# A two-layer recurrence on one core: all gates by ScalarE from PSUM, state copies and one forget product on VectorE, own places for the variances, another order

## The chip, the cores and the metric

The kernel runs on one core of one Trainium2 chip. The metric is the device time of one execution in microseconds (us); less is better.

## What is computed

The input is an image of 256 x 256 positions with 32 channels. Four layers follow each other, each adding to the image: an attention block (here only its value and gate paths matter, since the softmax runs over an axis of length 1), two Sobel layers, and a recurrent network. Each layer first normalizes the image by groups of channels. The change concerns the fourth layer alone. It reads the image as 256 sequences (rows) of 256 steps (columns), with a hidden size of 128 and two layers:

```
def step(carry, x_t):
    h_all, c_all = carry
    z = x_t @ W_lat + b_lat
    for j in range(L):
        zz = jnp.concatenate([z, h_all[j]], axis=1) @ W_cell[j] + b_cell[j]
        zz = _group_norm(zz, gn_gamma[j], gn_beta[j])
        i, f, o, g = jnp.split(zz, 4, axis=1)
        c = jax.nn.sigmoid(f) * c_all[j] + jax.nn.sigmoid(i) * jnp.tanh(g)
        h = jax.nn.sigmoid(o) * jnp.tanh(c)
        z = z + h
        ...
    x_hat = x_t + z @ W_out + b_out
```

The group norm has four groups of 128, which are the four gates, so each gate has its own mean and standard deviation per sequence. All data are float32.

## The kernel before

The first 640 us or so hold the input, the attention layer and the two Sobel layers. The change doesn't touch them.

The recurrence takes the rest. The 256 sequences are two halves of 128, one sequence per partition. So each time step has four units of work: layer `l` (0 or 1) and half `h` (0 or 1), written (0, 0), (0, 1), (1, 0) and (1, 1). The weights are centred beforehand, so the four gates' means are zero and only a variance is left to compute. Each unit consists of these parts, by the names of the program:

- `x` (line 763): the input's share of `zz`, a PSUM tile of 128 x 512 with all four gates, from `fx`. The function `project` issues it; two of them, for a unit of layer 0 and one of layer 1, are issued as a pair. Every unit has one PSUM buffer, so the next `x` of a unit has to wait until the last reader of its `zz` is done.
- `i` (line 788), for layer 1: adds layer 0's new state. `m` (line 793): adds the unit's own state of the step before.
- `sq` (line 801): ScalarE squares `zz` from PSUM. `rd` (line 806): VectorE sums the squares of each gate into `ve`. `pw` (line 809): GpSimd raises `ve` to the power -0.5; the result is `rs`, 1/std of four gates per sequence.
- `nz`, `n2` (line 773), for layer 0: VectorE multiplies `zz` by `rs`, in two halves of 256 columns, into `zn` in SBUF.
- The gates `ga`. In layer 0 ScalarE reads `zn`: `sg` (line 837) does two sigmoids at once, `so` (line 839) the third, `tg` (line 841) the tanh. In layer 1 ScalarE reads `zz` from PSUM with `rs` as the scale, one instruction for each gate (line 782).
- `ig` (line 844): VectorE multiplies input gate and tanh. `fc` (line 848): GpSimd multiplies forget gate and old `c`. `c` (line 852): VectorE adds the two. `th` (line 856): ScalarE takes tanh. `h` (line 859): VectorE multiplies by the output gate.
- `T` (line 864): TensorE transposes `h` into PSUM. `e` (line 869): the copy into `hT`, by VectorE in layer 0 and by ScalarE in layer 1. `hs` (line 874): GpSimd adds both layers' `hT` for the output.

After every block of four steps the output follows (`emit`): `px` from `xa` (line 880) and from `hs` (line 883) on TensorE, `fin` on ScalarE (line 891), a transpose `st` on VectorE (line 894), and four DMAs on SP's queue. SP also loads the next inputs, `xt`, well ahead.

The order of the instructions is written out by hand. `PLAN` gives each part of a unit a due time, and `PERIOD` is added for each step; `EMIT` does the same for the output. All parts of all steps are sorted by due time and issued in that order. The times serve for sorting only: each engine takes its own instructions in that order, and each waits for what it needs. An engine never overtakes.

There is a second arm of the program for general gamma and beta of the group norm, chosen at run time. With these inputs it isn't taken.

Of the kernel before, what the change touches and what calls it, by code (L numbers as in the profile page):

```python
# [10 lines left out]
F32 = mybir.dt.float32  # L11
AF = mybir.ActivationFunctionType
# [5 lines left out]
T = 256  # L18
C = 32
J = 4  # L20
NB = T // J
P = 128
H = 128
L = 2
# [633 lines left out]
class RecurrentInputs:  # L658
# [40 lines left out]

PERIOD = 8.665
PLAN = {
    (0, 0): dict(m=0.0, sq=1.54, rd=2.25, pw=3.0, nz=4.22, n2=4.58, sg=5.22, tg=5.54, fc=5.7),
    (0, 1): dict(m=4.42, sq=5.96, rd=6.66, pw=7.42, nz=8.53, n2=8.88, sg=9.47, tg=9.79, fc=9.95),
    (1, 0): dict(x=9.85, i=11.2, m=12.21, sq=13.35, rd=13.99, pw=14.81, nz=15.89, tg=15.9, so=16.2),
    (1, 1): dict(x=13.95, i=15.37, m=16.46, sq=17.59, rd=18.25, pw=19.07, nz=20.29, tg=20.3),
}
PLAN[0, 0].update(ig=5.95, c=6.4, so=6.5, th=6.75, h=7.28, T=7.65, e=8.01)
PLAN[0, 1].update(ig=10.2, c=10.65, so=10.75, th=11.0, h=11.53, T=12.06, e=12.62)  # L710
PLAN[1, 0].update(si=16.5, sg=16.8, ig=16.96, fc=17.27, c=17.89, th=18.66, h=19.09, T=19.71, e=20.07)
PLAN[1, 1].update(si=20.59, so=20.89, ig=21.05, sg=21.2, fc=21.66, c=22.25, th=23.08, h=23.51)
PLAN[1, 1].update(T=23.88, e=24.29, hs=30.77)
EMIT = 35.52


def recurrence(tc, out, ident, weights, inputs, general):

    nc = tc.nc
    wc, fx, e4, cst4, wout = weights  # L720
    sqs = inputs.sqs
    ctx = ExitStack()
# [15 lines left out]
                    nc.scalar.copy(dst[:, l, :], pb)  # L738

    up = ctx.enter_context(tc.tile_pool(name="unit", bufs=5))  # L740
    sp = ctx.enter_context(tc.tile_pool(name="state", bufs=2))
    hp = ctx.enter_context(tc.tile_pool(name="hid", bufs=6))
    op = ctx.enter_context(tc.tile_pool(name="outp", bufs=2))
# [6 lines left out]
    v = {}  # L750
    todo = []

    def at(when, what, *args):
        todo.append((when, len(todo), what, args))
# [10 lines left out]
    def one(name, l, h, t):  # L765
        seqs = slice(h * P, (h + 1) * P)
        get = lambda k: v[k, l, h]
        gates = lambda x, g: x[:, g * H : (g + 1) * H]
        four = lambda x: x.rearrange("p (g m) -> p g m", g=4)

        def half(i):
            g = slice(2 * i, 2 * i + 2)
            nc.vector.tensor_mul(  # L773
                four(get("zn"))[:, g, :],
                four(get("zz"))[:, g, :],
                get("rs")[:, g].unsqueeze(2).to_broadcast([P, 2, H]),
            )

        def gate(g, func):

            x, scale = (get("zn"), 1.0) if general else (get("zz"), get("rs")[:, g : g + 1])
            nc.scalar.activation(gates(get("ga"), g), gates(x, g), func, scale=scale)  # L782

        if name == "x":
            project(0, 1 - h, t + 1 + h)
            project(1, h, t)
        elif name == "i":
            nc.tensor.matmul(  # L788
                get("zz"), lhsT=v["hT", 0, t][:, seqs], rhs=wc[:, l, 0, :], start=False, stop=t == 0
            )  # L790
        elif name == "m":
            if t:
                nc.tensor.matmul(  # L793
                    get("zz"),
                    lhsT=v["hT", l, t - 1][:, seqs],
                    rhs=wc[:, l, 1, :],
                    start=False,
                    stop=True,
                )
        elif name == "sq":  # L800
            nc.scalar.activation(  # L801
                sqs[l, h][:, :, 0:H], four(get("zz")), AF.Square, scale=float(H**-0.5)
            )
        elif name == "rd":
            ve = v["ve", l, h] = up.tile([P, 4], F32, name="ve")
            nc.vector.tensor_reduce(ve, sqs[l, h], AX.X, ALU.add)  # L806
        elif name == "pw":
            rs = v["rs", l, h] = up.tile([P, 4], F32, name="rs")
            nc.gpsimd.tensor_tensor(rs, get("ve"), inputs.mhalf, ALU.pow)  # L809
        elif name == "n2":  # L810
            if not general:
                half(1)
        elif name == "nz":
            if l == 0 or general:
                zn = v["zn", l, h] = up.tile([P, 4 * H], F32, name="zn")
            if l:
                v["ga", l, h] = up.tile([P, 4 * H], F32, name="ga")
            if not general:
                if l == 0:
                    half(0)  # L820
                return
            for g in range(4):
                nc.vector.scalar_tensor_tensor(
                    gates(zn, g),
                    gates(get("zz"), g),
                    get("rs")[:, g : g + 1],
                    gates(gam[:, l, :], g),
                    ALU.mult,
                    ALU.mult,
                )  # L830
            nc.vector.tensor_add(zn, zn, bet[:, l, :])
        elif l and name in ("si", "sg", "so", "tg"):
            g = ("si", "sg", "so", "tg").index(name)
            gate(g, AF.Tanh if name == "tg" else AF.Sigmoid)
        elif name == "sg":
            ga = v["ga", l, h] = up.tile([P, 4 * H], F32, name="ga")
            nc.scalar.activation(ga[:, 0 : 2 * H], get("zn")[:, 0 : 2 * H], AF.Sigmoid)  # L837
        elif name == "so":
            nc.scalar.activation(gates(get("ga"), 2), gates(get("zn"), 2), AF.Sigmoid)
        elif name == "tg":  # L840
            nc.scalar.activation(gates(get("ga"), 3), gates(get("zn"), 3), AF.Tanh)
        elif name == "ig":
            c = v["cn", l, h] = sp.tile([P, H], F32, name=f"c{l}{h}")
            nc.vector.tensor_mul(c, gates(get("ga"), 0), gates(get("ga"), 3))  # L844
        elif name == "fc":
            if t:
                fc = v["fc", l, h] = up.tile([P, H], F32, name="fc")
                nc.gpsimd.tensor_mul(fc, gates(get("ga"), 1), get("c"))  # L848
        elif name == "c":
            c = get("cn")  # L850
            if t:
                nc.vector.tensor_add(c, c, get("fc"))  # L852
            v["c", l, h] = c
        elif name == "th":
            th = v["th", l, h] = up.tile([P, H], F32, name="th")
            nc.scalar.activation(th, get("c"), AF.Tanh)  # L856
        elif name == "h":
            hh = v["h", l, h] = up.tile([P, H], F32, name="h")
            nc.vector.tensor_mul(hh, gates(get("ga"), 2), get("th"))  # L859
        elif name == "hs":  # L860
            both(t)
        elif name == "T":
            pt = v["pt", l, h] = ps_h.tile([P, 4 * H], F32, name="pt")
            nc.tensor.transpose(pt[:, 0:P], get("h"), ident)  # L864
        elif name == "e":
            if h == 0:
                v["hT", l, t] = hp.tile([P, S], F32, name=f"hT{l}")
            copy = nc.scalar.copy if l else nc.vector.tensor_copy
            copy(v["hT", l, t][:, seqs], get("pt")[:, 0:P])  # L869

    def both(t):

# [2 lines left out]

    def emit(blk, part):

        if part == 0:
            px = v["px"] = ps_x.tile([P, S], F32, name="px")
            nc.tensor.matmul(px, lhsT=e4, rhs=inputs.xa[:, blk, :], start=True, stop=False)  # L880
        elif part == 1:
            for j in range(J):
                nc.tensor.matmul(  # L883
                    v["px"][j * C : (j + 1) * C, :],
                    lhsT=wout,
                    rhs=v.pop(("hs", blk * J + j)),
                    start=False,
                    stop=True,
                )
            fin = v["fin"] = op.tile([P, S], F32, name="fin")  # L890
            nc.scalar.activation(fin, v["px"], AF.Identity, bias=cst4)
        else:
            st = op.tile([P, S], F32, name="st")
            nc.vector.transpose(st, v["fin"])
            for j in range(J):
                nc.sync.dma_start(
                    out=out_q[j, :, blk],
                    in_=st[j * C : (j + 1) * C].rearrange("p (q c) -> p q c", c=C),
                )

    for k in range(inputs.NX, NB // inputs.XT):
        at(((k - inputs.NX + 1) * inputs.XT * J + 2.0) * PERIOD, inputs.load, k)
    for h in range(2):
        at(-1e5, project, 0, h, 0)
    at(PLAN[1, 1]["x"] - PERIOD, project, 0, 0, 1)
    for t in range(T):
# [1 line left out]
            for name, when in ops.items():  # L908
                at(t * PERIOD + when, one, name, l, h, t)
    for blk in range(NB):  # L910
        for part in range(3):
            at((blk * J + J - 1 + part) * PERIOD + EMIT, emit, blk, part)
    todo.sort(key=lambda e: e[:2])
    with tc.manual_schedule():
        for _, _, what, args in todo:
# [43 lines left out]
```

## Time and profile before

| What | Value |
|---|---|
| Three runs | 2893.24, 2894.18, 2903.16 us; median 2894.18 |
| The profiled execution | 2892.63 us |
| Its span, from first to last instruction | 2890.8 us |
| Mean granted TensorE clock | 0.983 |
| Busy, 1500 to 2000 us: PE, VectorE, ScalarE, GpSimd | 486.1, 427.9, 414.7, 372.1 us |
| One matmul pass, `L793` (two passes are one float32 matmul) | 594 ns |
| `rs` on GpSimd, `L809` | 1016 ns |
| `ve` on VectorE, `L806` | 678 ns |
| `sq` on ScalarE, `L801` | 591 ns |
| A gate from PSUM with `rs` as scale, `L782` | 371 ns |

The profile names an engine PE (TensorE matmuls), PEld (TensorE weight loads), DVE (VectorE), ACT (ScalarE), POOL (GpSimd) or SP. A row of the groups gives the line, engine and operation, what it writes and reads with shapes, how often, the busy time in us and the mean in ns of one, and then the idle time of the engine just before it with what ended most of that. A line of the timeline gives start, time taken, engine, line and operation; equal neighbours are merged ("x4"), and then the time taken runs from the first start to the last end. Neighbours on an engine can overlap, so a row's mean can be longer than the distance to the next start. The chain of work that ended last is followed back from the last instruction; in its answer in order of time each piece has its start, its length and the name of who held it. "issue" there is time in which nothing shown was waited for.

### The profile page before, as it was taken

To read this page: it belongs to the slowest core of one execution; us is meant where nothing else is said; L and a number is where in the kernel's file an instruction comes from. 1 tells how busy PE (TensorE), PEld (TensorE's weight loads), DVE (VectorE), ACT (ScalarE), POOL (GpSimd) and SP (SyncE) were. 2 spreads that over 40 slices of the span, in tenths; PEclk is the share of its full clock that TensorE was granted. 3 is DMA by queue.
4 is the path that set the end of the run, shared out by engine and by line. 5 is a ranking of instruction groups with operands and counts; after the bars stand their busy time and mean duration, and the time that the engine had idled before them with its cause. 6 is when DMAs were issued, how large, how long until landed. Compare 5 with 4: busy or idle time off the path is not lost.

```text
span 2890.8 us, 40872 instructions
## 1 busy us (share of the span) xinstructions
PE 2754.4 (95%) x9561; PEld 993.9 (34%) x9561; DVE 2422.5 (84%) x6507; ACT 2274.8 (79%) x6961; POOL 1934.2 (67%) x2586
## 2 busy tenths in 40 slices
PE   7899898989999999999999999999999999999997
PEld 4433333333333333333333333333333333333332
DVE  6788798978888888888888888888888888888886
ACT  5477676758888888888888888888888888888886
POOL 2311375657777777777777777777777777777775
PEclk9899999989999999999999999999999999999999
DMA  3000000000000000000000000000000000000000
GB/s 133 1 1 1 16 1 1 1 22 6 16 13 12 12 12 12 12 12 12 12 12 14 12 12 12 12 12 12 12 12 12 12 12 12 13 13 16 7 5 7
DMA packets 94354, 38.53 MB, mean 13 GB/s; under 512 B 74852, under 2 KB 91269, under 8 KB 94104
## 3 DMA queue, kind: packets, MB, share of 16 engines
q1 hardware_dynamic: 93156, 34.67, 5.3%
q8 instruction: 79, 1.29, 0.2%
q14 instruction: 171, 1.40, 0.2%
q10 hardware_dynamic: 148, 0.86, 0.1%
q0 software_dynamic: 800, 0.30, 0.0%
HBM read 10.63 MB, written 8.39 MB: 7 GB/s over the span
## 4 chain that ended last, share of the span: by engine, by line
PE 44%; DVE 32%; POOL 12%; issue 7%; ACT 2%; POOLq 0%; DVEq 0%; ACTq 0%
DVE ve L806 14%; POOL rs L809 11%; PE zz L793 11%; DVE c L852 7%; PE zz L788 6%; PE zz L763 5%; DVE zn L773 4%; PE pv L279 4%; PE pg L452 4%; PE pg L412 3%; DVE c L844 3%; PE pt L864 3%; PE pg L303 2%; PE px L883 2%; PE pg L279 1%
## 5 line engine op out<-in xcount | busy, mean ns | idle before, releaser
L809 POOL TENSOR_TENSOR rs<-ve,mhalf 128x4 f32<-128x4 f32 x1024 | 1040.3, 1016 | 252.0 <-DVE ve L806 225.5
L793 PE MATMUL zz<-wc,hT 128*128 128x512 f32 x2040 | 962.2, 594 | 1.2 <-DVE hT L869 1.2
L801 ACT ACTIVATE sq<-zz 128x512 f32<-128x512 f32 x1024 | 605.4, 591 | 245.7 <-PE zz L793 240.3
L806 DVE TENSOR_REDUCE ve<-sq 128x4 f32<-128x516 f32 x1024 | 694.4, 678 | 9.9 <-ACT sq L801 9.5
L848 POOL TENSOR_TENSOR fc<-ga,c 128x128 f32<-128x128 f32 x1020 | 464.8, 456 | 333.4 <-ACT ga L837 313.3
L782 ACT ACTIVATE ga<-zz,rs 128x128 f32<-128x128 f32 x2048 | 585.0, 371 | 4.6 <-POOL rs L809 1.1
L763 PE MATMUL zz<-fx,xt 33*128 33x512 f32 x2048 | 585.2, 643 | 3.3 <-issue 1.9
L788 PE MATMUL zz<-wc,hT 128*128 128x512 f32 x1024 | 525.3, 595 | 0.0
L793 PEld LDWEIGHTS zz<-wc,hT 128*128 128x128 f32 x2040 | 361.0, 197 | 262.6 <-DVE hT L869 201.6
L844 DVE TENSOR_TENSOR c<-ga 128x128 f32<-128x128 f32 x1024 | 307.5, 300 | 156.3 <-ACT ga L782 98.3
L773 DVE TENSOR_TENSOR zn<-zz,rs 128x256 f32<-128x256 f32 x1024 | 386.2, 419 | 54.8 <-POOL rs L809 20.4
L864 PEld LDWEIGHTS pt<-ident,h 128*128 128x128 f32 x1024 | 142.3, 139 | 797.9 <-DVE h L859 748.9
L864 PE MATMUL pt<-ident,h 128*128 128x128 f32 x1024 | 323.7, 316 | 67.4 <-DVE h L859 40.8
L856 ACT ACTIVATE th<-c 128x128 f32<-128x128 f32 x1024 | 310.4, 303 | 79.6 <-DVE c L852 59.8
L852 DVE TENSOR_TENSOR c<-c,fc 128x128 f32<-128x128 f32 x1020 | 368.8, 362 | 3.1 <-POOL fc L848 2.0
L859 DVE TENSOR_TENSOR h<-ga,th 128x128 f32<-128x128 f32 x1024 | 290.2, 283 | 0.8 <-ACT th L856 0.8
L763 PEld LDWEIGHTS zz<-fx,xt 33*128 33x128 f32 x2048 | 156.6, 185 | 348.2 <-PE zz L793 309.0
L869 DVE COPY hT<-pt 128x128 f32<-128x128 f32 x512 | 147.5, 288 | 111.5 <-PE pt L864 111.5
L837 ACT ACTIVATE ga<-zn 128x256 f32<-128x256 f32 x512 | 208.7, 408 | 3.9 <-DVE zn L773 3.9
L297 DVE TENSOR_TENSOR o<-pv,sg 128x512 f32<-128x512 f32 x256 | 158.0, 679 | 46.5 <-PE pg L279 37.7
L874 POOL TENSOR_TENSOR hs<-hT,hT 128x256 f32<-128x256 f32 x256 | 186.0, 726 | 1.7 <-ACT hT L869 1.7
L788 PEld LDWEIGHTS zz<-wc,hT 128*128 128x128 f32 x1024 | 183.3, 219 | 2.3 <-issue 2.3
(143 smaller groups left out, 2745.6 us busy)
## 6 DMA issues: line engine op xcount, KB each, us to landing
xt<-xa SPq DMA_DIRECT2D x256, 64.0 KB, 2.0
nat<-in_x_dram SPq DMA_DIRECT2D x16, 512.0 KB, 7.1
out_dram<-st SPq DMA_DIRECT2D x256, 32.0 KB, 1.7
wc<-in_L_conv_W_cell_dram SPq DMA_DIRECT2D x2, 512.0 KB, 4.5
kt<-in_consts_dram ACTq DMA_DIRECT2D x1, 832.0 KB, 5.9
wv<-in_L_conv_Wv_dram POOLq DMA_DIRECT2D x4, 32.0 KB, 5.0
wg<-in_L_conv_Wg_dram POOLq DMA_DIRECT2D x4, 32.0 KB, 6.0
gamma<-in_L_conv_ln_gamma_dram POOLq DMA_DIRECT2D x4, 0.1 KB, 6.3
```

Of the source, the lines that this page charges most:

```text
L763: nc.tensor.matmul(zz, lhsT=x, rhs=fx[rows, l, :], start=True, stop=l == 0 and t == 0)
L773: nc.vector.tensor_mul(four(get("zn"))[:, g, :], four(get("zz"))[:, g, :], get("rs")[:, g].unsqueeze(2).to_broadcast([P, 2, H]),)
L782: nc.scalar.activation(gates(get("ga"), g), gates(x, g), func, scale=scale)
L788: nc.tensor.matmul(get("zz"), lhsT=v["hT", 0, t][:, seqs], rhs=wc[:, l, 0, :], start=False, stop=t == 0)
L793: nc.tensor.matmul(get("zz"), lhsT=v["hT", l, t - 1][:, seqs], rhs=wc[:, l, 1, :], start=False, stop=True,)
L801: nc.scalar.activation(sqs[l, h][:, :, 0:H], four(get("zz")), AF.Square, scale=float(H**-0.5))
L806: nc.vector.tensor_reduce(ve, sqs[l, h], AX.X, ALU.add)
L809: nc.gpsimd.tensor_tensor(rs, get("ve"), inputs.mhalf, ALU.pow)
L844: nc.vector.tensor_mul(c, gates(get("ga"), 0), gates(get("ga"), 3))
L848: nc.gpsimd.tensor_mul(fc, gates(get("ga"), 1), get("c"))
L852: nc.vector.tensor_add(c, c, get("fc"))
L864: nc.tensor.transpose(pt[:, 0:P], get("h"), ident)
```

## The change

- Layer 0 takes its gates as layer 1 did: four activations from `zz` in PSUM with `rs` as scale. `zn` with its two VectorE products falls away (in the arm that is taken), and so does the double sigmoid. The parts are now called `sf`, `si`, `so`, `tg` in all units, and their order differs from unit to unit.
- The output gate gets a tile of its own, `go`, with three buffers.
- `e` is done by VectorE in both layers. `fc` is done by VectorE in layer 1 and stays on GpSimd in layer 0.
- `ve` and `rs` get places of their own for 64 steps, in two tiles that are never given back, in place of five rotating buffers.
- The plan has new due times for everything, and the output's four parts have due times of their own (`OUT`), with `fin` split from the matmuls ahead of it.

```diff
-PERIOD = 8.665
+SLOTS = 64
+PERIOD = 8.700
 PLAN = {
-    (0, 0): dict(m=0.0, sq=1.54, rd=2.25, pw=3.0, nz=4.22, n2=4.58, sg=5.22, tg=5.54, fc=5.7),
-    (0, 1): dict(m=4.42, sq=5.96, rd=6.66, pw=7.42, nz=8.53, n2=8.88, sg=9.47, tg=9.79, fc=9.95),
-    (1, 0): dict(x=9.85, i=11.2, m=12.21, sq=13.35, rd=13.99, pw=14.81, nz=15.89, tg=15.9, so=16.2),
-    (1, 1): dict(x=13.95, i=15.37, m=16.46, sq=17.59, rd=18.25, pw=19.07, nz=20.29, tg=20.3),
+    (0, 0): dict(m=3.34, sq=3.72, rd=4.73, pw=5.61, ga=5.84, sf=5.86, so=6.12, fc=6.24),
+    (0, 1): dict(m=7.00, sq=7.12, rd=8.38, pw=8.64, ga=9.88, sf=9.90, si=10.02, tg=10.28),
+    (1, 0): dict(x=13.81, i=17.21, m=17.59, sq=18.47, rd=19.23, pw=19.73, ga=21.35, sf=21.37),
+    (1, 1): dict(x=20.62, i=21.50, m=22.38, sq=23.14, rd=24.02, pw=25.15, ga=25.26, sf=25.28),
 }
-PLAN[0, 0].update(ig=5.95, c=6.4, so=6.5, th=6.75, h=7.28, T=7.65, e=8.01)
-PLAN[0, 1].update(ig=10.2, c=10.65, so=10.75, th=11.0, h=11.53, T=12.06, e=12.62)
-PLAN[1, 0].update(si=16.5, sg=16.8, ig=16.96, fc=17.27, c=17.89, th=18.66, h=19.09, T=19.71, e=20.07)
-PLAN[1, 1].update(si=20.59, so=20.89, ig=21.05, sg=21.2, fc=21.66, c=22.25, th=23.08, h=23.51)
-PLAN[1, 1].update(T=23.88, e=24.29, hs=30.77)
-EMIT = 35.52
+PLAN[0, 0].update(tg=6.37, si=6.75, ig=7.38, c=8.01, th=8.26, h=8.76, T=9.02, e=10.40)
+PLAN[0, 1].update(fc=10.65, so=11.16, ig=11.28, c=11.54, th=12.17, h=12.55, T=12.92, e=15.19)
+PLAN[1, 0].update(so=21.75, si=22.00, tg=22.25, fc=22.63, ig=22.76, c=22.88, th=23.39, h=24.27)
+PLAN[1, 0].update(T=24.90, e=25.03)
+PLAN[1, 1].update(tg=26.54, si=26.67, so=26.79, ig=26.92, fc=27.05, c=27.55, th=28.31, h=28.81)
+PLAN[1, 1].update(T=29.69, e=30.58, hs=34.23)
+
+OUT = dict(o0=29.06, o1=54.28, of=55.29, ot=68.15)
...
+    kp = ctx.enter_context(tc.tile_pool(name="norm", bufs=1))
+    sums = kp.tile([P, 2 * L, SLOTS, 4], F32, name="ve")
+    roots = kp.tile([P, 2 * L, SLOTS, 4], F32, name="rs")
...
             x, scale = (get("zn"), 1.0) if general else (get("zz"), get("rs")[:, g : g + 1])
-            nc.scalar.activation(gates(get("ga"), g), gates(x, g), func, scale=scale)
+            if g == 2:
+                v["go", l, h] = up.tile([P, H], F32, name="go", bufs=3)
+            dst = get("go") if g == 2 else gates(get("ga"), g)
+            nc.scalar.activation(dst, gates(x, g), func, scale=scale)
...
         elif name == "rd":
-            ve = v["ve", l, h] = up.tile([P, 4], F32, name="ve")
+            ve = v["ve", l, h] = sums[:, 2 * l + h, t % SLOTS, :]
             nc.vector.tensor_reduce(ve, sqs[l, h], AX.X, ALU.add)
         elif name == "pw":
-            rs = v["rs", l, h] = up.tile([P, 4], F32, name="rs")
+            rs = v["rs", l, h] = roots[:, 2 * l + h, t % SLOTS, :]
             nc.gpsimd.tensor_tensor(rs, get("ve"), inputs.mhalf, ALU.pow)
...
-        elif l and name in ("si", "sg", "so", "tg"):
-            g = ("si", "sg", "so", "tg").index(name)
+        elif name in ("si", "sf", "so", "tg"):
+            g = ("si", "sf", "so", "tg").index(name)
             gate(g, AF.Tanh if name == "tg" else AF.Sigmoid)
-        elif name == "sg":
-            ga = v["ga", l, h] = up.tile([P, 4 * H], F32, name="ga")
-            nc.scalar.activation(ga[:, 0 : 2 * H], get("zn")[:, 0 : 2 * H], AF.Sigmoid)
-        elif name == "so":
-            nc.scalar.activation(gates(get("ga"), 2), gates(get("zn"), 2), AF.Sigmoid)
-        elif name == "tg":
-            nc.scalar.activation(gates(get("ga"), 3), gates(get("zn"), 3), AF.Tanh)
...
-                nc.gpsimd.tensor_mul(fc, gates(get("ga"), 1), get("c"))
+                eng = nc.vector if l else nc.gpsimd
+                eng.tensor_mul(fc, gates(get("ga"), 1), get("c"))
...
-            nc.vector.tensor_mul(hh, gates(get("ga"), 2), get("th"))
+            nc.vector.tensor_mul(hh, get("go"), get("th"))
...
-            copy = nc.scalar.copy if l else nc.vector.tensor_copy
-            copy(v["hT", l, t][:, seqs], get("pt")[:, 0:P])
+            nc.vector.tensor_copy(v["hT", l, t][:, seqs], get("pt")[:, 0:P])
...
     for blk in range(NB):
-        for part in range(3):
-            at((blk * J + J - 1 + part) * PERIOD + EMIT, emit, blk, part)
+        for part, when in OUT.items():
+            at((blk * J + J - 1) * PERIOD + when, emit, blk, part)
```

More of the change, by code (lines that the diff above doesn't have):

```diff
@@ L769, in one @@
         four = lambda x: x.rearrange("p (g m) -> p g m", g=4)
[L771 to L777, printed above, removed]
         def gate(g, func):
             x, scale = (get("zn"), 1.0) if general else (get("zz"), get("rs")[:, g : g + 1])
-            nc.scalar.activation(gates(get("ga"), g), gates(x, g), func, scale=scale)
+            if g == 2:
+                v["go", l, h] = up.tile([P, H], F32, name="go", bufs=3)
+            dst = get("go") if g == 2 else gates(get("ga"), g)
+            nc.scalar.activation(dst, gates(x, g), func, scale=scale)
         if name == "x":
@@ L804, in one @@
         elif name == "rd":
-            ve = v["ve", l, h] = up.tile([P, 4], F32, name="ve")
+            ve = v["ve", l, h] = sums[:, 2 * l + h, t % SLOTS, :]
             nc.vector.tensor_reduce(ve, sqs[l, h], AX.X, ALU.add)
         elif name == "pw":
-            rs = v["rs", l, h] = up.tile([P, 4], F32, name="rs")
+            rs = v["rs", l, h] = roots[:, 2 * l + h, t % SLOTS, :]
             nc.gpsimd.tensor_tensor(rs, get("ve"), inputs.mhalf, ALU.pow)
-        elif name == "n2":
+        elif name == "ga":
+            v["ga", l, h] = up.tile([P, 4 * H], F32, name="ga")
             if not general:
[L812 to L820, printed above, removed]
                 return
+            zn = v["zn", l, h] = up.tile([P, 4 * H], F32, name="zn")
             for g in range(4):
@@ L876, in emit @@
     def emit(blk, part):
-        if part == 0:
+        if part == "o0":
             px = v["px"] = ps_x.tile([P, S], F32, name="px")
             nc.tensor.matmul(px, lhsT=e4, rhs=inputs.xa[:, blk, :], start=True, stop=False)
-        elif part == 1:
+        elif part == "o1":
             for j in range(J):
@@ L889, in emit @@
                 )
+        elif part == "of":
             fin = v["fin"] = op.tile([P, S], F32, name="fin")
```

## The prediction, made before the result was known

> I call the four units of a time step A (layer 0, first half of the sequences), B (layer 0, second half), C and D (layer 1, first and second half).
>
> **What bounds the kernel now.** I read the page first: busy shares and the chain of work that ended last.
>
> ```profile
> PE 2754.4 (95%) x9561; PEld 993.9 (34%) x9561; DVE 2422.5 (84%) x6507; ACT 2274.8 (79%) x6961; POOL 1934.2 (67%) x2586
> ...
> PE 44%; DVE 32%; POOL 12%; issue 7%; ACT 2%; POOLq 0%; DVEq 0%; ACTq 0%
> DVE ve L806 14%; POOL rs L809 11%; PE zz L793 11%; DVE c L852 7%; PE zz L788 6%; PE zz L763 5%; DVE zn L773 4%; PE pv L279 4%; PE pg L452 4%; PE pg L412 3%; DVE c L844 3%; PE pt L864 3%; PE pg L303 2%; PE px L883 2%; PE pg L279 1%
> ```
>
> PE looks full, yet the chain goes as much through VectorE and GpSimd (ve, rs, c, zn) as through the recurrence's matmuls. The shares mix stages, so next the stretches: the recurrence runs from about 640 to 2866 us, evenly.
>
> ```profile
> 1500.00:2000.00 500.00, 486.11 (x1527) 169.71 (x1526) 427.86 (x1276) 414.74 (x1391) 372.13 (x517) 1.00 0.06 12
> ```
>
> The columns are PE, PEld, DVE, ACT, POOL, then the granted clock (1.00). In the groups of 1500 to 2366 us, ve stands 398 times in 866 us; at four a step that is 8.70 us per step, 34.8 per block of four steps. In the timeline a step without output takes 2000.13 to 2008.65 = 8.52. Then the chain in order of time, over half a step:
>
> ```profile
> 2008.69 0.41 DVE zn L773
> 2009.10 0.47 DVE c L852
> 2009.58 0.60 DVE ve L806
> ...
> 2010.52 0.28 DVE c L852
> 2010.80 0.61 DVE ve L806
> ...
> 2011.54 1.02 POOL rs L809
> 2012.56 0.02 issue
> ```
>
> It begins with zn at 2008.35 and ends with the other half's zn at 2012.58: 4.23 us, twice 8.46 a step. This loop is the bound: VectorE without a break from zn to ve (3.06), the hand-over (0.13), rs on GpSimd (1.02). PE isn't in it. How much PE has left is seen in its timeline, where the starts count and the modelled ends don't:
>
> ```profile
> 2000.88 1.13 PE L763 MATMUL zz<-fx,xt 33*128 33x512 f32 x4
> 2002.13 0.33 PE L864 MATMUL pt<-ident,h 128*128 128x128 f32 x1
> 2002.29 1.02 PE L788 MATMUL zz<-wc,hT 128*128 128x512 f32 x2
> 2003.15 0.30 PE L864 MATMUL pt<-ident,h 128*128 128x128 f32 x1
> 2003.29 1.88 PE L793 MATMUL zz<-wc,hT 128*128 128x512 f32 x4
> 2005.11 1.13 PE L763 MATMUL zz<-fx,xt 33*128 33x512 f32 x4
> ```
>
> A matmul of 512 columns is two passes; four passes in 1.88 with 0.59 for the last gives (1.88-0.59)/3 = 0.43 a pass, 0.86 a matmul. A transpose costs 0.16 (2002.13 to 2002.29). A pair of x matmuls takes 1.06 (656.41 to the transpose at 657.47, where it didn't wait) plus 0.09 ahead of it (2003.29 + 4 x 0.43 = 5.01 against 5.11). Per step: six matmuls 5.16, four transposes 0.64, two pairs 2.30: 8.10. A block adds px from xa, 0.43 (2858.11 to 2858.64 without the 0.09), and px from hs, 0.56 (2865.93 to 2866.49): 0.25 a step. So **PE needs 8.35 of 8.70 us**, and 0.35 x 256 = 90 us is all that any change off PE can win: about 2806.
>
> **What the Trainium skill says.** "SBUF — State Buffer", section "Who interferes with whom": a VectorE instruction with two SBUF inputs contends with a GpSimd instruction that reads SBUF, and the first to issue blocks the other for its whole length. The trace agrees: c at 2000.50 takes 0.55 beside hs (2000.18 to 2000.91) and ends 0.147 after it, against 0.28 alone; ve isn't affected (0.68). "ScalarE: Activation LUTs", section "What ACT_TABLE_LOAD costs": a [128,1] pointer operand adds about 93 ns, and back-to-back activations overlap by about as much. Here a gate with rs as scale takes 0.371 against 0.30 without, and four take 1.14, so (1.14-0.37)/3 = 0.26 apart (0.25 by their starts). "TensorE: Matmul & The Clock Gate", section "Architectural detail": TensorE pulls weight loads ahead of running matmuls. The trace agrees: a load for L793 at 2003.84 stands beside matmuls that run until 2004.15. So a wait that ends somewhat early costs PE nothing.
>
> **The change part by part.** Rows:
>
> ```profile
> L809 POOL TENSOR_TENSOR rs<-ve,mhalf 128x4 f32<-128x4 f32 x1024 | 1040.3, 1016 | 252.0 <-DVE ve L806 225.5
> L806 DVE TENSOR_REDUCE ve<-sq 128x4 f32<-128x516 f32 x1024 | 694.4, 678 | 9.9 <-ACT sq L801 9.5
> L848 POOL TENSOR_TENSOR fc<-ga,c 128x128 f32<-128x128 f32 x1020 | 464.8, 456 | 333.4 <-ACT ga L837 313.3
> L782 ACT ACTIVATE ga<-zz,rs 128x128 f32<-128x128 f32 x2048 | 585.0, 371 | 4.6 <-POOL rs L809 1.1
> L773 DVE TENSOR_TENSOR zn<-zz,rs 128x256 f32<-128x256 f32 x1024 | 386.2, 419 | 54.8 <-POOL rs L809 20.4
> L837 ACT ACTIVATE ga<-zn 128x256 f32<-128x256 f32 x512 | 208.7, 408 | 3.9 <-DVE zn L773 3.9
> ```
>
> Layer 0's gates from PSUM: VectorE loses 4 zn a step at 0.34 apart, 1.36. It gains two state copies (0.21 apart; row of L869, 288 ns) and two fc (as h, 283 ns, 0.20 apart): 0.82. Most of what leaves stood in the loop, and rs then releases ScalarE directly. The loop is gone.
>
> ScalarE: sixteen gates at 0.25, four sq at 0.49 (2000.13 to 2000.62), four tanh at 0.20 (2001.13 to 2001.33), fin 0.37/4: 6.9 a step, of 8.35. Lone gates between other activations aren't shown; bounds are 0.25 (as in a run) and 0.371 (no overlap). I take 0.25, since mixed neighbours overlap too (sq of 0.597 is followed after 0.49).
>
> GpSimd loses two fc (0.91): 5.7 left. VectorE's new fc costs 0.20 free, up to 0.55 if it meets hs; it saves layer 1 a hand-over. I take 0.20, on neither critical chain.
>
> Own places for ve and rs: one wait per rs where there were two in every second; ve's start to rs is 0.76 with one (2000.98 to 2001.73), 0.82 with two (2002.20 to 2003.02). At most 2 x 0.06 a step, zero where rs isn't next. I count it in the chain below. As rs and ve don't block their old readers here, nothing queues for it.
>
> Order: zz is now held until the last gate, so C's x pair, with B's inputs in it, waits for C's tg; behind it on PE stand B's m, C's transpose and the rest. The PE order in the built program is x(B,C), Bm, CT, Ci, Cm, AT, x(A,D), Am, DT, Di, BT, Dm. Output keeps its work; px stands ahead of x(A,D), where PE pays it in full; fin and st fall in gaps of ScalarE and VectorE (st cost 0.36 inside the old loop). The output DMAs stay on SP, later by steps; input loads are issued 12 steps ahead of use, so SP is no limit.
>
> I laid one step of the new order on all engines by these spacings, x(B,C) at 0: Bm 1.05, CT 1.91, Cm 2.94, AT 3.80, Am 5.11, DT 5.97, Dm 7.15, next pair 8.10. Links: m to sq 1.06 (2003.29 to 2004.35), sq to ve 0.63, ve to rs 0.76, rs to gate 1.04, gate to its reader 0.41, c to tanh 0.31, tanh to h 0.34, h to transpose 0.34, transpose to copy 0.34, copy to m 0.34. The two tight waits:
> - DT. From Bm: 1.06 + 0.63 + 0.76 + 1.04, B's sf and si 0.50, tg 0.25 (D's tanh is queued behind it), then 0.34 + 0.34 = 4.92. PE from Bm to DT: 4.92. No slack; a transpose that waited ends 0.03 later.
> - x(B,C). From Am: sq at 1.06, 0.19 later behind B's tanh, 0.48, three gates 0.75, the fourth 0.37, release 0.05 = 2.90; PE's way is 2.99.
> The others: A's copy to Am 0.35 free, BT 0.15, AT 0.12, D's copy to Dm 0.11.
>
> So a plain step is 8.10 + 0.03, and 0.03 more for waits that near: 8.16; with output 8.41. Against 8.70: -0.285 x 256 = -73 us. The order is deeper (D's m 2.2 steps after A's, before 1.9): at most +2. The profiled execution took 2892.6 (span 2890.8 and 1.8 around it); minus 71 is 2821.6. The runs' median is 1.6 above it: **2823**.
>
> **The rivals.**
> - *Small waits add up* (0.15): BT, AT, Dm and the x pair each lose 0.1 as their slacks are overdrawn. Plain step 8.45, output half hidden in these waits: 8.60, -24 + 2: 2872. For: four slacks under 0.16. Against: a late step gives the other engines time.
> - *The port lock moves onto B's chain* (0.12), slower. hs is issued once D's rs ends, at 2.55 to 2.60; A's state add starts at 2.46, right behind C's copy. Lead 0.1. If hs goes first, the add ends 0.147 after it, 3.47 instead of 2.74; B's ve, queued behind, starts at 3.39 instead of 2.75, and DT is 0.65 late. Step 8.78, output hidden: +0.085 x 256 + 2 = +24: 2918. It decides as soon as hs is issued ahead of the add. For: c met hs in every step before (0.55 to 0.78). Against: the lead holds whenever x(B,C) starts undelayed.
> - *Gates don't overlap away from runs* (0.04), slower: at 0.371 ScalarE takes 5.94 + 1.96 + 0.80 + 0.09 = 8.79 a step, 2919. Against: the mixed overlaps named.
> - *No change* (0.05): small waits, and the lock in some steps only; about 2893.
>
> **How the numbers follow.** The forecast has 0.64: from PE's floor, 2806, a little below for errors in it, to about 2846. With 0.15 for small waits, up to about 2878, 0.79 is covered; the range must go slightly into no change: 2800 to 2890. About 0.5%, 14 us, is what a measurement can tell here. Faster by more: 0.64 + 0.15 = 0.79; within: 0.05; slower: 0.12 + 0.04 = 0.16.
>
> **What would show it.** PE's starts in a plain step 8.1 to 8.2 apart, with transposes and x pairs hardly waiting; the chain mostly PE and ScalarE, no zn; L782's successor at 0.25 apart; c beside hs rare. Wrong if DT waits long for h (follow it back: ve of B behind a stretched c is the lock; late gates are ScalarE), or if granted clock falls below 1.00.

## The result, and the profile after

| | us |
|---|---|
| Kernel before, four runs on the same chip | median 2896.08 (2893.24 to 2903.16) |
| Kernel after, four runs | median 2881.20 (2880.13 to 2884.80) |
| Ratio | 0.9949, 95% interval 0.9936 to 0.9961 |
| Profiled execution of after; its span | 2880.13; 2878.2 |

The change wins 15 us where 71 were forecast. One of the four runs of e10 below took 3935.85 us at a granted clock of 0.65 and is left out; in all other runs the granted clock was 0.96 to 0.98.

The page of the kernel after: busy shares, then the chain that ended last by engine and by line.

```profile
PE 2776.8 (96%) x9561; PEld 1034.1 (36%) x9561; DVE 2401.1 (83%) x6505; ACT 2369.6 (82%) x6961; POOL 1722.2 (60%) x2076
PE 76%; DVE 9%; POOL 7%; ACT 5%; issue 1%; DVEq 0%; POOLq 0%; ACTq 0%
```

The old loop is gone: PE holds 76% of the chain where it held 44%, and no `zn` is left. But some 20% of the chain still goes through other engines. Half steps of the recurrence, from one pair of x matmuls to the next over a block of four steps (eight half steps), are 4.06, 4.92, 4.06, 4.47, 4.21, 4.06, 4.21, 4.63, together 34.62 us; before the change a block took 34.79. Difference -0.17 x 64 blocks = -11 us of the 15 measured. The shortest, 4.06, are the forecast's PE floor (8.10/2). Two are 0.43 and 0.57 longer because they hold px. Two of 4.21 lose 0.15 each at a transpose that waits. That leaves 0.43 in the second and 0.41 in the fourth to be explained. The chain in order of time through the half step of 4.47:

```profile
2007.94 0.60 ACT sq L803
2008.54 0.28 ACT ga L784
...
2008.89 0.46 POOL fc L837
...
2009.34 1.02 POOL rs L811
...
2010.38 0.82 DVE c L841
2011.20 0.60 DVE ve L808
2011.80 0.21 DVE h L848
...
2012.05 0.33 PE pt L853
```

The chain leaves PE at 2007.92 and comes back at 2012.05, with A's transpose. The odd piece is `c` (line 841), A's state add, with 0.82 us. The timeline shows what stands beside it:

```profile
2007.84 1.13 PE L770 MATMUL zz<-fx,xt 33*128 33x512 f32 x4
2010.33 0.72 POOL L862 TENSOR_TENSOR hs<-hT,hT 128x256 f32<-128x256 f32 x1
2010.38 0.82 DVE L841 TENSOR_TENSOR c<-c,fc 128x128 f32<-128x128 f32 x1
```

And the same place two half steps later, in the next step of the same trace:

```profile
2016.52 1.13 PE L770 MATMUL zz<-fx,xt 33*128 33x512 f32 x4
2019.06 0.28 DVE L841 TENSOR_TENSOR c<-c,fc 128x128 f32<-128x128 f32 x1
2019.10 0.83 POOL L862 TENSOR_TENSOR hs<-hT,hT 128x256 f32<-128x256 f32 x1
```

Take the starts relative to the x pair. The add comes at 2010.38 - 2007.84 = 2.54 both times. hs comes at 2.49 the first time and at 2.58 the second. Whoever is issued first runs at its own length, and the other is stretched: the add from 0.28 to 0.82, or hs from 0.72 to 0.83. This is what the section "Who interferes with whom" of "SBUF — State Buffer" in the Trainium skill says (who issues first blocks the other), seen from both sides; the time lost is somewhat less than the overlap with the first, 0.54 of 0.67 and 0.11 of 0.24. Counted over the trace, hs goes first in steps 2 and 3 of each block and the add in steps 0 and 1, with three exceptions in the 253 steps in which the two meet. The group of line 841 has the average of both:

```profile
L841 DVE TENSOR_TENSOR c<-c,fc 128x128 f32<-128x128 f32 x1020 | 361.6, 355 | 18.4 <-DVE hT L857 0.5
```

Of 1020 adds, half the steps' A adds are stretched by 0.54: 128 x 0.54 = 69 us. 361.6 - 1020 x 0.288 (their mean where none is stretched, run e11 below) = 68. A mean of 355 ns hides that it is one add in eight.

**Theory 1:** the time lost is this lock, twice a block. It is 0.42 to 0.43 us each time, 0.84 x 64 = 54 us; without it the kernel would be at about 2881 - 54 = 2827, close to the forecast of 2823. **Rivals:** the lock is only a symptom and the small waits on PE (D's transpose above all) would take its place; or one part of the change costs what another wins: fc or the copies on VectorE, or ScalarE's gates.

### The profile page after: what moved, and what is told of

The parts are those of the page before. It is cut to its first block, busy times and chain, and to the rows that moved or that the text cites. A ratio compares the mean times of both kernels' runs of the same rounds, so it can differ in the third digit from the quotient of the medians.

```text
span 2878.2 us, 38258 instructions
## 1 busy us (share of the span) xinstructions
PE 2776.8 (96%) x9561; PEld 1034.1 (36%) x9561; DVE 2401.1 (83%) x6505; ACT 2369.6 (82%) x6961; POOL 1722.2 (60%) x2076
## 4 chain that ended last, share of the span: by engine, by line
PE 76%; DVE 9%; POOL 7%; ACT 5%; issue 1%; DVEq 0%; POOLq 0%; ACTq 0%
PE zz L795 26%; PE zz L770 15%; PE zz L790 11%; PE pt L853 5%; POOL rs L811 4%; PE pv L279 4%; PE pg L452 4%; DVE c L841 4%; PE pg L412 3%; DVE ve L808 3%; ACT sq L803 3%; PE pg L303 2%; POOL fc L837 2%; ACT ga L784 1%; PE px L871 1%; PE pg L279 1%
## 5 line engine op out<-in xcount | busy, mean ns | idle before, releaser
L795 PE MATMUL zz<-wc,hT 128*128 128x512 f32 x2040 | 1102.3, 622 | 0.0
L784 ACT ACTIVATE ga<-zz,rs 128x128 f32<-128x128 f32 x3072 | 986.5, 368 | 29.1 <-POOL rs L811 9.9
L790 PE MATMUL zz<-wc,hT 128*128 128x512 f32 x1024 | 524.5, 594 | 0.0
L795 PEld LDWEIGHTS zz<-wc,hT 128*128 128x128 f32 x2040 | 324.5, 188 | 555.6 <-DVE hT L857 399.0
L848 DVE TENSOR_TENSOR h<-go,th 128x128 f32<-128x128 f32 x1024 | 309.5, 302 | 96.9 <-ACT th L845 96.9
L784 ACT ACTIVATE go<-zz,rs 128x128 f32<-128x128 f32 x1024 | 378.8, 370 | 0.0
L837 POOL TENSOR_TENSOR fc<-ga,c 128x128 f32<-128x128 f32 x510 | 232.2, 455 | 244.0 <-ACT ga L784 244.0
L841 DVE TENSOR_TENSOR c<-c,fc 128x128 f32<-128x128 f32 x1020 | 361.6, 355 | 18.4 <-DVE hT L857 0.5
L853 PE MATMUL pt<-ident,h 128*128 128x128 f32 x1024 | 294.3, 287 | 36.3 <-DVE h L848 36.2
L857 DVE COPY hT<-pt 128x128 f32<-128x128 f32 x1024 | 293.2, 286 | 10.2 <-PE pt L853 2.7
L862 POOL TENSOR_TENSOR hs<-hT,hT 128x256 f32<-128x256 f32 x256 | 198.1, 774 | 2.5 <-DVE hT L857 2.5
L790 PEld LDWEIGHTS zz<-wc,hT 128*128 128x128 f32 x1024 | 162.4, 198 | 68.2 <-issue 56.4
L294 ACT ACTIVATE sg<-pg 128x512 f32<-128x512 f32 x256 | 138.6, 599 | 31.0 <-PE pg L279 25.0
```

The costliest lines, as they stand in the source:

```text
L784: nc.scalar.activation(dst, gates(x, g), func, scale=scale)
L790: nc.tensor.matmul(get("zz"), lhsT=v["hT", 0, t][:, seqs], rhs=wc[:, l, 0, :], start=False, stop=t == 0)
L795: nc.tensor.matmul(get("zz"), lhsT=v["hT", l, t - 1][:, seqs], rhs=wc[:, l, 1, :], start=False, stop=True,)
L848: nc.vector.tensor_mul(hh, get("go"), get("th"))
```

## The experiments

Each ratio is to the kernel before, run on the same chip.

**e1, the add ahead of its neighbour.** A's add is put ahead of C's copy in VectorE's order.

```diff
-PLAN[0, 0].update(tg=6.37, si=6.75, ig=7.38, c=8.01, ...
+PLAN[0, 0].update(tg=6.37, si=6.75, ig=7.38, c=7.60, ...
```

> The changed kernel with one due time moved: the state add of unit (0, 0) stands ahead of the copy of unit (1, 0) on VectorE, not behind it. Theory 1 (port lock): in the changed kernel hs on GpSimd is issued 0.05 us ahead of that add and holds it for 0.82 us; ve of (0, 1) and h of (0, 0) stand behind it, so the transpose of (0, 0) comes 0.4 us late. Issued ahead of hs, the add takes 0.28, the plain step falls towards the 8.26 us of the steps before the first hs, and the time to 2840 to 2858 us. Theory 2 (TensorE itself is full: the matmul after an x pair takes 0.1 us longer than I counted, twice a step, and the rest is its own work): 2875 to 2885 us, as without the edit.

2840.37 us, ratio 0.9803 (0.9787 to 0.9820). The add now starts 2.37 or 2.46 after the x pair, ahead of hs in every step, and 41 us are won by one due time. It falls short of the next two by 11 to 13 us: C's copy, pushed behind the add, comes 2.58 or 2.67 after the x pair instead of 2.33. Where it comes at 2.67, the weights of C's m are loaded only as it starts, and it takes 0.97 to the next instruction, not 0.86.

**e2, no hs.** hs is computed in the first step only, and all outputs use that sum: 255 sums are left out.

```diff
-        hs = v["hs", t] = hp.tile([P, S], F32, name="hs")
-        nc.gpsimd.tensor_add(hs, ...)
+        if t == 0:
+            v["hs0"] = kp.tile([P, S], F32, name="hs")
+            nc.gpsimd.tensor_add(v["hs0"], ...)
+        v["hs", t] = v["hs0"]
```

> The changed kernel without hs on GpSimd: the sum of both layers' states is made in the first step only, and the output of every step is projected from that one sum, so 255 sums are left out. Theory 1 (port lock): nothing on GpSimd reads long enough beside the adds; plain step 8.26, time 2838 to 2855 us. Theory 2 (TensorE full): 2875 to 2885 us.

2827.38 us, ratio 0.9764 (0.9748 to 0.9781), 11 us below the range of the expectation, which took 8.26 for every step, px apart; two of four in a block take 8.11 here. With the partner of the lock gone, 53.8 us are won.

**e3, hs behind B's rs.** All work is kept; hs is moved behind the next instruction on GpSimd.

```diff
-PLAN[1, 1].update(T=29.69, e=30.58, hs=34.23)
+PLAN[1, 1].update(T=29.69, e=30.58, hs=34.76)
```

> The changed kernel with the due time of hs moved behind rs of (0, 1) on GpSimd, by one place. Theory 1 (port lock): hs then runs about 2 us later, where VectorE has a copy from PSUM and ve, which it doesn't hold; the forget product of (0, 1) and rs of (1, 0) come up to 0.4 us later behind it: 2842 to 2865 us. Theory 2 (TensorE full): 2875 to 2885 us.

2829.03 us, ratio 0.9765 (0.9749 to 0.9782), also below its expected range. hs now runs beside ve, which isn't affected by it (0.688 on average, 0.687 in the kernel after), and A's add has 0.28 us. 52.2 us come back, all but 1.6 of what leaving hs out brings. The chain of e3 in order of time, two half steps without px and without a wait, and the start of the next:

```profile
2009.28 1.06 PE zz L770 x4
...
2013.34 1.06 PE zz L770 x4
...
2017.39 1.10 PE zz L770 x4
```

8.11 us, with nothing but PE in between; PE holds 94% of the page's chain. A block's half steps are 4.49, 4.06, 4.06, 4.21, 4.05, 4.22, 4.63, 4.06: 33.78 us, against 34.62 with the lock. The 0.84 between them are the 54 us. This is the fastest version with all its work in this study, faster than both kernels.

**e11 and e12, hs moved in two steps of four.** The sharpest form of the same test. e11 moves hs in steps 2 and 3 of a block, where it locked the add; e12 (with `t % 4 < 2`) in steps 0 and 1, where the add came first anyway.

```diff
-                at(t * PERIOD + when, one, name, l, h, t)
+                late = 0.53 if name == "hs" and t % 4 >= 2 else 0.0
+                at(t * PERIOD + when + late, one, name, l, h, t)
```

> The kernel after, with hs behind B's rs only in the steps 2 and 3 of each block of four, the ones in which it locked A's add. If these two collisions are the whole loss, the time is that of the kernel with hs moved in all steps: 2826 to 2836 us. If hs weighs on the other two steps as well (0.83 us long there), between 2840 and 2870 us.

> The counterpart: hs behind B's rs only in the steps 0 and 1 of each block, in which the add came first anyway. If only the two locked steps cost, nothing is won: 2876 to 2886 us. If hs's length beside VectorE matters wherever it stands, half of the gain: 2850 to 2865 us.

e11: 2832.34 us, ratio 0.9781 (0.9764 to 0.9797); e12: 2881.50, ratio 0.9952 (0.9935 to 0.9968). The two steps hold the whole loss, and an hs stretched to 0.83 in the other two costs nothing that can be measured.

**e9, own places undone.** If the lock is a race over 0.05 us, then anything that delays hs by that much removes it, a slower rs too. The kernel after, with `ve` and `rs` back in five rotating buffers, hs where the change has it:

```diff
-            rs = v["rs", l, h] = roots[:, 2 * l + h, t % SLOTS, :]
+            rs = v["rs", l, h] = up.tile([P, 4], F32, name="rs")
```

(and `ve` likewise)

> The kernel after, with ve and rs back in rotating buffers and hs left where the change has it (behind layer 0's fc on GpSimd, ahead of A's state add in time by 0.05 us in two steps of four). Theory 1, the lock is a race of hs (+2.49 us after the x pair) against A's add (+2.54): each rs now starts some 0.05 us later, so hs comes at +2.54 or later and the add is mostly first. Undoing this part of the change then makes the kernel faster than the one after: 2838 to 2855 us. Theory 2, hs keeps its lead over the add in the two steps, since the add's own inputs shift as well: the 10 us that own places are worth come on top, 2880 to 2895 us.

2840.58 us, ratio 0.9811 (0.9795 to 0.9828): taking an improvement away makes the kernel 40.6 us faster. From its timeline (the x pair of this step is at 2009.85):

```profile
2012.38 0.28 DVE L838 TENSOR_TENSOR c<-c,fc 128x128 f32<-128x128 f32 x1
2012.41 0.85 POOL L859 TENSOR_TENSOR hs<-hT,hT 128x256 f32<-128x256 f32 x1
```

Over the whole trace the add is at 2.54 as before, and hs at 2.56 in the steps 2 and 3, so that 0.02 us decide; in the steps where it is latest hs comes at 2.65. Theory 2 of the expectation, 2880 to 2895, falls.

**e6, the same with hs out of the way.** e3, with rotating buffers for `ve` and `rs`.

> The version without the lock, with ve and rs in five rotating buffers as before the change. Each rs then has a second wait, for an earlier rs. My sum gave it 0.06 us where rs is on the path; it is on the chain to the transpose of (1, 1), that has no slack: 2830 to 2846 us. The rival, that the second wait is over before the first and costs nothing: 2826 to 2832 us.

2838.69 us, ratio 0.9790 (0.9774 to 0.9807). Without the race, own places win 9.7 us over rotating ones (2838.69 - 2829.03, from two chips; by the ratios 0.0025 x 2896 = 7). That is near the limit of what these runs can tell, as the two intervals overlap, but the trace agrees: the half steps in which D's transpose waits take 4.28 instead of 4.21, twice a block, 0.063 x 2 x 64 = 8 us. So the same edit wins some 10 us or loses 41, by where hs stands.

**e5, D's transpose made early.** The forecast held D's transpose to be the tightest wait. In e3, D's tanh and h are put ahead of B's tg and ig.

```diff
-PLAN[1, 1].update(..., c=27.55, th=28.31, h=28.81)
+PLAN[1, 1].update(..., c=27.55, th=27.60, h=28.60)
```

> The changed kernel with hs behind rs of (0, 1) (the version without the lock) and one edit more: ScalarE does the tanh of the state of (1, 1) ahead of tg of (0, 1), and VectorE its h ahead of ig of (0, 1). In the version without the lock TensorE is at work for 33.78 us a block; without waits it needs 4 x 8.11 + 1.0 = 33.4. The rest are the halves of 4.21 us, where the transpose of (1, 1) waited. If that wait is the one left, the block falls to 33.5 and the time to 2806 to 2820 us. The rival: tg and with it c, tanh and sq of the next units come 0.2 us later, C's gates then hold up the x pair: 2825 to 2850 us.

2855.41 us, ratio 0.9854 (0.9838 to 0.9871), 5 us above even the rival's range and 26 us worse than e3: what is pushed back on ScalarE and VectorE is B's. B's transpose now waits (0.28 us in the chain where a free one has 0.11), and D's copy, queued on VectorE behind B's h, is too late for the weights of D's m to be loaded ahead (1.00 in the chain, 0.86 in e3). The order of the change is the better compromise; the wait moves, and is longer where it lands.

**e4, the gates alone.** The kernel before with layer 0's four gates from PSUM at the place of the old double sigmoid, nothing else moved.

```diff
-            ga = v["ga", l, h] = up.tile([P, 4 * H], F32, name="ga")
-            nc.scalar.activation(ga[:, 0 : 2 * H], get("zn")[:, 0 : 2 * H], AF.Sigmoid)
+            gate(1, AF.Sigmoid)
+            gate(0, AF.Sigmoid)
...
-    (0, 0): dict(..., sg=5.22, tg=5.54, fc=5.7),
+    (0, 0): dict(..., sg=5.22, tg=5.23, so=5.24, fc=5.7),
```

> The kernel before with one part of the change: layer 0 takes its four gates from PSUM with rs as scale, all four together where sg stood, since the next x pair overwrites zz; zn falls away; all else, the order too, is as before. Theory 1 says that the loop over zn was the bound and is gone, so the kernel gains where nothing else is late: 2830 to 2870 us. The rival: the x pair, issued right behind, now waits for the fourth gate, 1.12 us after rs, so the loop goes on over ScalarE and TensorE: rs ended at 2004.04 in the trace of before, the gates would end at 5.20 and x start at 5.25 instead of 5.11, 0.14 later in each half step: 2890 to 2970 us.

3199.01 us, ratio 1.1045 (1.1026 to 1.1063): both expectations missed. The chain of e4 in order of time has a new loop, here over one turn:

```profile
2005.36 1.13 PE zz L763 x4
...
2007.72 0.88 PE zz L793 x2
...
2008.61 0.60 ACT sq L801
2009.21 0.30 ACT ga L782 x2
...
2009.61 0.64 ACT ga L782 x2
```

The next x pair starts at 2010.29: 4.93 us per half step. `zz` is now held until the last gate of layer 0, so the x pair waits for ScalarE; layer 0's gates stand behind layer 1's sq on ScalarE; that sq waits for layer 1's m; and that m is queued on PE behind the x pair. In the old order the gates from PSUM close a loop through two queues. So the gates win nothing without the new order, which puts them ahead of that sq.

**e7 and e10, layer 1's fc on GpSimd again.** e7 is e3 with

```diff
-                eng = nc.vector if l else nc.gpsimd
+                eng = nc.gpsimd
```

> The version without the lock, with layer 1's forget product on GpSimd as before the change. Theory 1: two more instructions a step of 0.46 us that read SBUF on GpSimd, and rs queued behind them; where VectorE's products meet them they wait as for hs: 2835 to 2875 us. The rival, that slack takes it: 2826 to 2834 us.

3217.24 us, ratio 1.1101 (1.1082 to 1.1119), 388 us above e3 and far outside the expectation. Its chain in order of time:

```profile
2006.49 1.01 POOL rs L811
2007.49 0.69 POOL hs L862
2008.19 0.42 POOL fc L837
...
2008.63 0.53 DVE c L841
2009.16 0.21 DVE hT L857
```

With hs behind B's rs, fc for D's state waits on GpSimd behind hs, D's add is locked by the fc that follows (0.53 instead of 0.28), and A's copy, queued behind the add, comes late: PE stands idle for 0.93 before A's m at 2009.41. The granted clock adds to it: in 43 half steps it falls to half for a stretch (704.7 to 708.1 us: 0.53 on average), and these take 7.18 us where the others at the same place take 5.64, 43 x 1.54 = 66 us. So e7 tests several things at once. e10 takes fc and hs apart: fc on GpSimd, with hs behind those fc (hs=36.76).

> The kernel after with layer 1's fc on GpSimd again, and hs moved to the place behind both C's, D's and B's fc and ahead of C's rs (hs=36.76). Against the earlier run with fc on GpSimd and hs ahead of D's fc (3217 us). If the cost there came from hs standing between rs and fc (0.69 us on the way to D's state), 2840 to 2900 us. If fc on GpSimd itself is the cost (0.46 us instead of 0.20, two rs or fc queued ahead of it, and D's add locked behind it), over 3000 us.

2950.76 us, ratio 1.0195 (1.0175 to 1.0216). It lies between the two expectations: 266 of the 388 us came with hs's place, 66 of these with the lower clock, which e10 hardly shows; 122 are fc itself and what queues with it. In e10's chain the path from sq to PE still goes by ve, rs, fc (0.43), D's add and A's copy in two steps of each block. Even that is 57 us above the kernel before; in this order fc on VectorE is a needed part of the change.

**e8, layer 1's state copies on ScalarE again.** In e3.

```diff
-            nc.vector.tensor_copy(v["hT", l, t][:, seqs], get("pt")[:, 0:P])
+            copy = nc.scalar.copy if l else nc.vector.tensor_copy
+            copy(v["hT", l, t][:, seqs], get("pt")[:, 0:P])
```

> The version without the lock, with layer 1's state copies on ScalarE as before the change. ScalarE gains 0.5 us a step and has 1.2 free, but the copies stand between gates: C's gates have 0.09 us of slack before the x pair, and the copy of (1, 1) is queued inside them, so the pair waits some 0.16 to 0.25 us a step: 2850 to 2895 us. The rival, that the slack takes it since TensorE is the bound: 2826 to 2834 us.

3004.29 us, ratio 1.0363 (1.0346 to 1.0381), beyond its expectation. The copy of D's state stands on ScalarE behind A's sq (0.60 in the chain) and two of C's gates (0.26 each), and D's m behind the copy. D's m starts 0.56 after B's transpose (2000.84 to 2001.40 in e8), where e3 has 0.11, and takes another 0.1 since the weights aren't loaded ahead. The half steps with D's m are 0.55 longer than in e3, those with C's m 0.14: 4 x 0.69 x 64 = 177 us, the 175 measured. The expectation priced what the copy holds up among the gates, not what holds up the copy. On an engine with sixteen gates a step, a copy that releases PE is in the wrong queue.

## Why the prediction was wrong in its size

**What held.**
- *The bound.* The loop over zn, VectorE and rs is gone, and PE's floor is what the forecast said: a step in e3 without px and without waits takes 8.11 us (8.10 worked out). That it comes so close is partly luck, as the sum had two errors that cancel: the matmul behind an x pair takes 0.97 to the transpose behind it, not 0.86, and a transpose that doesn't wait takes 0.11, not 0.16. Two and four of them in a step: +0.22 - 0.20.
- *The small waits.* A block in e3 has 33.78 us, the forecast 4 x 8.41 = 33.64. The excess over PE's own 8 x 4.055 + 0.43 + 0.57 = 33.44 sits in two half steps of 4.21. The rival of small waits (2872) isn't seen, but e5 shows how near it is.
- *The forecast without the lock.* 2823 against 2829 measured in e3, 2827 in e2.
- *Gates overlap away from runs.* A single gate at 2007.44 in e3 is followed by a tanh at 2007.69, 0.25 later, though it takes 0.36 by itself. The rival at 2919 is out.
- *Own places.* At most 0.12 a step, 31 us, was stated as the bound; 7 to 10 measured (0.03 to 0.04 a step) where nothing else moves.
- *Prices of moved parts.* fc and the copies fit on VectorE; e7, e8 and e10 show that in this order each had to move.

**The step that failed** is the one that gave the lock's rival its low chance: "hs is issued once D's rs ends, at 2.55 to 2.60; A's state add starts at 2.46, right behind C's copy. Lead 0.1." with "the lead holds whenever x(B,C) starts undelayed". Measured, the add starts at 2.54 and hs at 2.49 or 2.58. Both terms were off by less than 0.1, and to the wrong sides:
- The add is 0.08 late, because C's transpose stands behind the matmul that follows the x pair and is at 2.02, not 1.91 (the cancelling error above doesn't cancel here, as C's is the first transpose after it); C's copy is then at 2.33, not 2.25, and the add 0.21 behind it.
- hs is 0.06 early in two steps. There A's fc starts at 1.05 after the x pair, and D's rs directly behind it at 1.51; in the other two steps A's own rs ends 0.09 later, and fc starts at 1.14 and D's rs at 1.55. So the lead isn't kept by an x pair that starts undelayed, as the forecast had it. It is lost just there: the half step ahead of that pair takes 4.06 where the lock follows, and 4.21, with D's transpose waiting, where it doesn't.

The first could have been bounded. In the order of before a transpose follows the x pair, so the trace showed no m there; the forecast carried over the 0.43 of passes behind other matmuls, with no range. A lead of 0.1 that rests on such a number isn't a lead.

**The rival's mechanism was right, its place and price only in part.** It was taken to hold up B's ve and by that D's transpose, 0.65 late in every step with the output hidden. B's ve is late, but what PE meets first is A's h, queued behind that ve on VectorE: A's transpose, some half step earlier. There the delay is 0.43 of PE's time, because A's transpose had slack; px is paid on top; and the lock falls in two steps of four. So 54 us are taken from a gain of 67 to 69 (e3 and e2 against before), and the rest is the 15 measured: the change ends between "no change" and faster, not slower. The case "no change" named "the lock in some steps only", but at 0.05 and together with small waits; which steps, and that the small waits stay away, it didn't say.

What parts the steps shows in the trace of after, first in a step with px ahead of x(A,D) on PE, then in one without:

```profile
2003.25 0.60 PE L868 MATMUL px<-xa,e 128*128 128x256 f32 x2
2004.84 1.12 PE L795 MATMUL zz<-wc,hT 128*128 128x512 f32 x2
2005.61 0.31 ACT L845 ACTIVATE th<-c 128x128 f32<-128x128 f32 x1 [0.31 <-DVE c L841]
2006.00 0.60 ACT L803 ACTIVATE sq<-zz 128x512 f32<-128x512 f32 x1
...
2021.68 1.12 PE L795 MATMUL zz<-wc,hT 128*128 128x512 f32 x2
2022.84 0.31 ACT L845 ACTIVATE th<-c 128x128 f32<-128x128 f32 x1 [0.31 <-DVE c L841]
2023.06 0.58 ACT L803 ACTIVATE sq<-zz 128x512 f32<-128x512 f32 x1
```

With px, A's sq starts 1.16 after A's m; without, 1.38, queued behind B's tanh, and A's rs ends 0.66 after the next x pair instead of 0.57. Over the trace hs goes first in all 125 steps with a px ahead of x(A,D), and the add in 126 of the 128 without one, among them step 2 of the first block, before any px has been issued. So the output's matmuls, which hold PE back while the other engines go on, fit as the cause. This is read from traces; it stays open as far as no run without the output was made.

## What to carry to other kernels

Where two engines that block each other are issued within 0.1 us of each other, a forecast to within 0.1 us can't say who goes first: price both outcomes, follow each through what is queued behind the loser, and take the pair apart in the order before anything else. A change that makes one step faster can lose such a race elsewhere (own places: up to 10 us won or 41 lost), so read the starts of both partners relative to one anchor, step by step, since a mean over the group hides that one in eight is stretched. And when work moves to another engine, ask what queue its result stands in: gates, fc and copies each cost 100 to 300 us in the wrong queue (e4, e10, e8), while with all three in place the two half steps of e3 shown above hold nothing but PE's own work.

## What the runs showed of the hardware

- Blocking isn't even-handed in price. The short add loses 0.54 us behind the long hs (it ends 0.15 after it), the long hs only 0.11 behind the short add. A start 0.02 to 0.05 us earlier decides.
- A float32 matmul of 512 columns takes 0.97 us to the next instruction on PE when its weight load begins with it, and 0.85 to 0.86 when the load ran ahead. Behind the x pair (two matmuls of 33 rows each for two units) the load never ran ahead, though the weights were there (B's copy ends at 2008.48 in the trace of after, load and matmul both start at 2008.89). So the advance of weight loads, for which the prediction named the skill's "TensorE: Matmul & The Clock Gate", section "Architectural detail", has an exception here; why, no run shows.
- A transpose costs PE 0.11 us where its input is ready in time, against 0.16 where the trace of before showed it.
- PE's busy share misleads near its bound: after stands at 494 of 500 us (1500 to 2000 us) and e3 at 500, though e3 needs 2.4% less for the same block.
